# Fill and emptying of a three-stage pipeline over groups: vectors loaded as rows, two groups side by side at the start, the last-but-one product in pieces at the end

## The chip, the cores and the metric

One core of a Trainium2 chip. The metric is the device time of one execution in microseconds (us), median of several executions. Batches of kernels ran on one chip beside fresh runs of the kernel before, whose median was 3388.9 to 3390.4 us each time. Ratios are the mean time of one kernel's runs over the mean of the other's runs of the same rounds, so they are not quite the ratio of the medians quoted here. The experiments ran in three batches (e1 to e4, e5 to e8, e9 to e12), each on another chip, and the changed kernel in a batch before them; since the kernel before itself moved by 1.5 us between batches, a difference of under 2 us between kernels of two batches is not shown by their medians alone.

## The reference, cut to what matters

64 graphs with 256 nodes and 256 features go through a graph attention layer and then a relational attention layer, in float32.

```python
def _gat(h, adj, W, a, out_features):            # called twice
    Wh = jnp.matmul(h, W)
    e = Wh @ a[:F] + swapaxes(Wh @ a[F:], 1, 2)
    scores = jnp.where(adj > 0, leaky_relu(e, 0.2), NEG)
    return jnp.matmul(softmax(scores, axis=1), Wh)

# layer 0
h = _gat(_gat(x, adj, W1, a1), adj, W2, a2)
h = layernorm(x + h, g_ln1, b_ln1)
x = layernorm(h + relu(h @ w_ff1 + b_ff1) @ w_ff2 + b_ff2, g_ln2, b_ln2)
# layer 1: 8 heads, value matrix chosen by the edge's relation r
q, k = x @ Wq + bq, x @ Wk + bk
attn = softmax(q @ k.T / sqrt(32))
out  = sum over r of (attn * (adj == r)) @ (x @ Wv[r] + bv[r])
x = layernorm(x + out @ Wo + bo, g1, beta1)
return layernorm(x + gelu(x @ W1 + b1) @ W2 + b2, g2, beta2)
```

## The kernel before

Two graphs are a group; there are 32 groups. A `turn` works on three groups at once: the relational layer of group y, the feed-forward part of the graph layer of group y+1, and the first part of the graph layer of group y+2. The order on TensorE is the order in which the program is written; the other engines are ordered by the framework, and each then runs its list strictly in that order (the traces below show it: VectorE stands for 8.84 us at one instruction while later ones are ready).

Names in the traces: a name that ends in p is a result of TensorE that another engine then reads or copies. aTp and xTp are transposes of the adjacency and of x; xpp is the projection by W; `rows` spreads a column of scores over all rows for the softmax; hpp and ygp are the first and the second attention sum of the graph layer; h1T, h2T and h3T are transposes after a norm; h1p and yfp are the two products of a feed-forward part; qp, kp, vp, sp, po, zo and yop are the steps of the relational layer. "Half clock" is a granted TensorE clock of 0.50, as the profile's windows give it.

The loads of the weights, and the loop:

```python
def column(v, name):                 # a vector as a column: one element per partition
    t = const.tile([P, n], F32, name=name)
    nc.scalar.dma_start(t, v.rearrange("(c p) -> p c", p=P))
# weight() and row() also start their transfers from nc.scalar
...
nc.vector.tensor_tensor(wv[:, :, 1, :], wv[:, :, 1, :], wv[:, :, 0, :], ALU.subtract)
nc.vector.tensor_tensor(rbv[:, F:], rbv[:, F:], rbv[:, :F], ALU.subtract)
...
nc.gpsimd.tensor_add(rb1, rb1, rbf2); nc.gpsimd.tensor_add(rb2, rb2, rbo); nc.gpsimd.tensor_add(rb3, rb3, rbt2)
...
def turn(y_, x_, z):
    hT = to_features(Y["y"], f"h2T{y_}", lg2, lb2)    # transposes; VectorE copies
    second_sums(x_)                                   # ygp, then norm
    q, k_ = queries_keys(y_, hT); v = values(...)     # qp, kp, vp
    h1hT = to_features(X["y"], f"h1T{x_}", lg1, lb1)
    # scores (sp) and applied (po, zo) of y between blocks of x's hidden product (h1p)
    early(z)                                          # aTp, xTp
    out_(0); project(z); out_(1); first_scores(z)     # yop, xpp, rows
    yf = hidden_out(x_, ...)                          # yfp of the graph layer
    hT = to_features(yn, f"h3T{y_}", lg3, lb3)
    Z["hp"] = gat_first(z, ...)                       # hpp
    h1 = hidden(y_, 1, hT, ...); second_scores(z)     # h1p of the relational layer, rows
    yf = hidden_out(y_, 1, h1, w2, res)               # yfp of the relational layer
    # norm, affine, one store for all four blocks of the group

for u in range(-2, NG):
    turn(u, u + 1, u + 2)            # turns -2 and -1: fill; turns 30 and 31: emptying
```

## Time and profile before

| | us |
|---|---|
| median of 4 runs | 3389.53 |
| span of the profiled run | 3388.5 |
| 32 steady turns of 102.31 | 3273.9 |
| everything else (start, fill, emptying, tail) | 114.6 |

The steady turns have no gap on TensorE, so the table's last row is all that the change can touch. A turn's start is read from the first transpose named h2T of its group in TensorE's timeline: 224.7 us for turn 1. The prediction below shows the page, the waits and ScalarE's queue. Here is the last turn of the kernel before, from TensorE's timeline; the columns are start, duration, engine, line, operation, out<-in, shape, count, and in brackets the idle time ahead of it with what ended it.

```profile
3322.71 1.94 PE L724 MATMUL po<-e,v 128*32 128x256 f32 x16 [6.72 <-DVE oT L734]
...
3333.98 3.63 PE L617 MATMUL yop<-wo,oT 128*128 128x256 f32 x8 [2.69 <-DVE oT L734]
3341.24 2.21 PE L540 MATMUL h3T31p<-ident,yo 128*128 128x128 f32 x8 [3.63 <-DVE yo L637]
3343.50 16.01 PE L655 MATMUL h1p<-h3T,w 128*128 128x512 f32 x32
```

Three waits for VectorE, and after them matmuls that run wholly or partly at half clock (0.50 in the windows from 3322 to 3326 and from 3342 to 3346 us): yop takes 3.63 us where it otherwise takes 1.89, and h1p 16.01 where it otherwise takes 13.90.

### The profile page before, as it was taken

The numbers are of one execution on the slowest core, as the hardware profiler recorded it, in microseconds if no ns is written. First come the engines' busy times: TensorE is split into PE (matmuls) and PEld (weight loads), VectorE is DVE, ScalarE is ACT, GpSimd is POOL, SyncE is SP. The second block draws the span as 40 slices with busy tenths as digits, with TensorE's granted clock in tenths as the row PEclk, the third lists the DMA queues.
The fourth block names the chain that finished last, engine by engine and source line by source line (L and its number), as shares of the span: only waits on it lengthen the run. The fifth ranks groups of instructions, "written<-read, shape, count | busy, mean of one in ns | idle before, by whom it ended". The sixth has DMA issues, their size and how long they took to land.

```text
span 3388.5 us, 43264 instructions
## 1 busy us (share of the span) xinstructions
PE 3304.7 (98%) x17946; PEld 2164.6 (64%) x17946; DVE 1820.3 (54%) x3607; ACT 1083.8 (32%) x1920; POOL 986.0 (29%) x844
## 2 busy tenths in 40 slices
PE   5899999999999999999999999999999999999996
PEld 3566666666666666666666666666666666666654
DVE  2545565545565555565455565455665455655444
ACT  1323333323323323323323333323333233333221
POOL 1233232332232332322332322332322332323321
PEclk7999999999999999999999999999999999999998
DMA  4000000000000000000000000000000000000000
GB/s 123 13 20 13 13 19 19 13 19 7 19 20 20 13 19 7 19 20 19 13 19 7 20 19 20 13 19 7 20 19 14 19 17 9 19 19 7 7 7 8
DMA packets 62458, 60.92 MB, mean 18 GB/s; under 512 B 7216, under 2 KB 61616, under 8 KB 62256
## 3 DMA queue, kind: packets, MB, share of 16 engines
q1 hardware_dynamic: 33792, 33.56, 3.1%
q0 software_dynamic: 16896, 16.78, 2.2%
q10 hardware_dynamic: 11568, 7.76, 0.9%
q8 instruction: 143, 2.34, 0.3%
q14 instruction: 59, 0.48, 0.0%
HBM read 41.31 MB, written 16.78 MB: 17 GB/s over the span
## 4 chain that ended last, share of the span: by engine, by line
PE 96%; DVE 1%; ACTq 1%; DMA 0%; issue 0%; POOL 0%; ACT 0%; POOLq 0%; DVEq 0%
PE h1p L655 27%; PE yfp L617 26%; PE po L724 7%; PE vp L687 6%; PE sp L703 4%; PE yop L617 3%; PE hpp L606 3%; PE kp L674 3%; PE ygp L617 3%; PE qp L674 3%; PE xpp L568 3%; PE zo L727 2%; PE rows L578 1%; PE aTp L555 1%; ACTq L462 1%
## 5 line engine op out<-in xcount | busy, mean ns | idle before, releaser
L655 PE MATMUL h1p<-h1T,wf 128*128 128x512 f32 x1024 | 474.6, 607 | 0.1
L655 PE MATMUL h1p<-h3T,w 128*128 128x512 f32 x1024 | 447.2, 595 | 1.0 <-DVE h3T L544 0.9
L617 PE MATMUL yfp<-wf,h 128*128 128x256 f32 x2048 | 447.3, 379 | 0.0
L617 PE MATMUL yfp<-w,h 128*128 128x256 f32 x2048 | 447.3, 379 | 0.0
L711 DVE TENSOR_TENSOR ea<-e,aT 128x1024 f32<-128x1024 f32 x256 | 320.2, 1291 | 195.2 <-ACT e L709 195.2
L617 PEld LDWEIGHTS yfp<-w,h 128*128 128x128 f32 x2048 | 386.8, 190 | 52.2 <-issue 1.0
L617 PEld LDWEIGHTS yfp<-wf,h 128*128 128x128 f32 x2048 | 386.7, 190 | 51.3
L709 ACT ACTIVATE e<-sp 128x512 f32<-128x512 f32 x512 | 264.3, 603 | 298.6 <-PE sp L703 298.6
L655 PEld LDWEIGHTS h1p<-h3T,w 128*128 128x128 f32 x1024 | 195.1, 191 | 234.4 <-issue 229.8
L733 POOL TENSOR_TENSOR low<-low,rz 128x512 f32<-128x512 f32 x64 | 82.2, 1284 | 880.3 <-DVE rz L732 880.3
L655 PEld LDWEIGHTS h1p<-h1T,wf 128*128 128x128 f32 x1024 | 184.9, 190 | 232.8 <-issue 190.9
L587 DVE SCALAR_TENSOR_TENSOR s<-s 128x512 f32<-128x512 f32 x128 | 90.2, 706 | 442.5 <-ACT s L584 441.3
L620 DVE TENSOR_TENSOR yf<-yfp,res 128x512 f32<-128x512 f32 x128 | 88.5, 692 | 424.9 <-PE yfp L617 423.8
L645 POOL TENSOR_TENSOR res<-res,rb 128x1024 f32<-128x1024 f32 x128 | 301.4, 2354 | 10.0
L657 ACT ACTIVATE h<-h1p,bf 128x512 f32<-128x512 f32 x256 | 177.3, 693 | 282.9 <-PE h1p L655 282.9
L657 ACT ACTIVATE h<-h1p,b 128x512 f32<-128x512 f32 x256 | 175.8, 687 | 258.7 <-PE h1p L655 257.5
L633 POOL TENSOR_TENSOR rs<-ve,mhalf 128x4 f32<-128x4 f32 x128 | 130.8, 1022 | 408.2 <-DVE ve L632 408.2
L732 DVE RECIPROCAL rz<-zo 128x512 f32<-128x512 f32 x64 | 214.6, 3354 | 63.8 <-PE zo L727 63.8
L687 PE MATMUL vp<-wv,h2T 128*128 128x512 f32 x512 | 230.1, 592 | 0.0
L676 ACT ACTIVATE q<-qp,bq 128x512 f32<-128x512 f32 x64 | 44.0, 688 | 530.8 <-PE qp L674 530.8
L608 ACT COPY hp<-hpp 128x258 f32<-128x258 f32 x128 | 48.0, 375 | 441.7 <-PE hpp L606 441.7
L644 POOL TENSOR_TENSOR res<-yf,rg 128x1024 f32<-128x1024 f32 x64 | 150.8, 2356 | 95.8 <-DVE yf L637 94.3
(486 smaller groups left out, 4393.1 us busy)
## 6 DMA issues: line engine op xcount, KB each, us to landing
xs<-in_x_dram SPq DMA_DIRECT2D x32, 512.0 KB, 3.9
af<-in_adj_dram POOLq DMA_DIRECT2D x32, 512.0 KB, 4.4
out_dram<-res SPq DMA_DIRECT2D x32, 512.0 KB, 2.9
wf<-in_L_gnn_w_ff_dram ACTq DMA_DIRECT2D x2, 1024.0 KB, 10.6
w<-in_L_gnn_W_dram ACTq DMA_DIRECT2D x2, 1024.0 KB, 9.6
wv<-in_L_gnn_Wv_dram ACTq DMA_DIRECT2D x2, 256.0 KB, 4.6
gw<-in_L_gnn_W_dram ACTq DMA_DIRECT2D x1, 256.0 KB, 4.5
gw2e<-in_L_gnn_W_dram ACTq DMA_DIRECT2D x1, 256.0 KB, 6.8
```

The costliest lines, as they stand in the source:

```text
L617: nc.tensor.matmul(ps[:, i * F:(i + 1) * F], lhs(t, k), rhs(b, k), start=(k == 0), stop=(k == n - 1))
L644: nc.gpsimd.tensor_mul(r, xn, g[:, None, :].to_broadcast([P, T, F]))
L645: nc.gpsimd.tensor_add(r, r, b[:, None, :].to_broadcast([P, T, F]))
L655: nc.tensor.matmul(ps, wi[:, k, f * P:(f + 1) * P], hT[:, k, :], start=(k == 0), stop=(k == KB - 1))
L657: nc.scalar.activation(h1[:, f, :], ps, func, bias=bi[:, f:f + 1])
L674: nc.tensor.matmul(ps, w[:, k, m * P:(m + 1) * P], hT[:, k, :], start=(k == 0), stop=(k == KB - 1))
L687: nc.tensor.matmul(ps, hT[:, k, t * P:(t + 1) * P], wvf[:, k, :], start=(k == 0), stop=(k == KB - 1))
L703: nc.tensor.matmul(ps[a][:, j * N:(j + 1) * N], k_[hp, m, j0:j0 + P], q[hp, m, b * N:(b + 1) * N], start=True, stop=True)
L709: nc.scalar.activation(e[:, a, :], ps[a], AF.Exp, scale=isd)
L711: nc.vector.tensor_tensor(ea[:, a:a + 2, :], e[:, a:a + 2, :], ab[:, None, :].to_broadcast([P, 2, NB * N]), ALU.mult)
L724: nc.tensor.matmul(po[hp, m * N:(m + 1) * N], vs[:, hp], w[:, a, j * N:(j + 1) * N], start=(n == 0), stop=(n == len(terms) - 1))
L732: nc.vector.reciprocal(rz, zo)
```

## The change

Its intent: take away what the two ends of the pipeline lose.

1. Loads. Vectors that were loaded as columns come as contiguous rows, twelve of them, and two small TensorE transposes turn them. Weights and bias rows are issued by SyncE instead of ScalarE. Group 1's data are loaded at once.
2. Fill. Groups 0 and 1 go through the first part of the graph layer side by side, so that the softmax of one can lie beside the matmuls of the other.
3. Emptying. Turn 30 does not do its last product; turn 31 does it in four pieces, at places where it used to wait.
4. Tail. The last group's sum, norm, affine and store are done for each half.

```diff
-        nc.scalar.dma_start(t, w.rearrange("(c p) f -> p c f", p=P))
+        nc.sync.dma_start(t, w.rearrange("(c p) f -> p c f", p=P))
...
-    def column(v, name):
-        nc.scalar.dma_start(t, v.rearrange("(c p) -> p c", p=P))
+    def columns(vs, name, queue):
+        for v, n in zip(vs, ns):
+            queue.dma_start(rows[at:at + n, :], v.rearrange("(c p) -> c p", p=P))
+        nc.tensor.transpose(ps[:, :at], rows[:at, :], ident[:at, :at])
+        nc.vector.tensor_copy(t, ps[:, :at])
...
+    def out_pieces(u, h1, res):          # a generator: one block of yfp per call,
+        ...                              # after two blocks: add, norm, affine, store
...
+                yield piece, None        # in turn(): ahead of apply 0 and of apply 2 ...
+            piece()                      # ... ahead of yop(1) and of h3T
...
+        if y_ == NG - 2:
+            left.append(out_pieces(y_, h1, res))
+        elif y_ == NG - 1:
+            for _ in out_pieces(y_, h1, res):
+                pass
...
-        for u in range(-2, NG):
+        for stage in (early, project, first_scores):
+            stage(0)
+        for stage in (early, project, first_scores):
+            stage(1)
+        for stage in (first_sums, second_scores):
+            stage(0)
+        for stage in (first_sums, second_scores):
+            stage(1)
+        second_sums(0)
+        hT = to_features(g[0]["y"], "h1T0", lg1, lb1)
+        h1 = hidden(0, 0, hT, wf1, bf1, AF.Relu, range(FB))
+        yf = hidden_out(0, 0, h1, wf2, g[0]["res"])
+        ...
+        second_sums(1)
+        for u in range(NG):
             turn(u, u + 1, u + 2)
```

More of the change, by code (lines that the diff above doesn't have):

```diff
@@ L429, in load @@
         nc.sync.dma_start(xs, x[G * u:G * (u + 1)].rearrange("b (c p) f -> p (b c) f", p=P))
-        af = io.tile([P, T, N], F32, tag="af", name=f"af{u}", bufs=1)
+        if u == 1:
+            af = work.tile([P, FB, TN], F32, tag="h1", name=f"af{u}", bufs=1)
+            af = af[:, 0:2, :].rearrange("p c (t n) -> p (c t) n", t=2)
+        else:
+            af = io.tile([P, T, N], F32, tag="af", name=f"af{u}", bufs=1)
         nc.gpsimd.dma_start(af, adj[G * u:G * (u + 1)].rearrange("b (c p) f -> p (b c) f", p=P))
         return xs, af
-    loaded = {0: load(0)}
     ident = const.tile([P, P], F32, name="ident")
@@ L455, in weight @@
         t = const.tile([P, w.shape[0] // P, w.shape[1]], F32, name=name)
-        nc.scalar.dma_start(t, w.rearrange("(c p) f -> p c f", p=P))
+        nc.sync.dma_start(t, w.rearrange("(c p) f -> p c f", p=P))
         return t
-    def column(v, name):
-        n = v.shape[0] // P
-        t = const.tile([P, n], F32, name=name)
-        nc.scalar.dma_start(t, v.rearrange("(c p) -> p c", p=P))
-        return t
+    def columns(vs, name, queue):
+        ns = [v.shape[0] // P for v in vs]
+        rows = work.tile([P, KB * N], F32, tag="rz", name=f"{name}r")[:, 0:P]
+        t = const.tile([P, sum(ns)], F32, name=name)
+        at, views = 0, []
+        for v, n in zip(vs, ns):
+            queue.dma_start(rows[at:at + n, :], v.rearrange("(c p) -> c p", p=P))
+            views.append(t[:, at:at + n])
+            at += n
+        ps = bank(f"{name}p")
+        nc.tensor.transpose(ps[:, :at], rows[:at, :], ident[:at, :at])
+        nc.vector.tensor_copy(t, ps[:, :at])
+        return views
     def row(v, name):
@@ L467, in row @@
         t = const.tile([P, n], F32, name=name)
-        nc.scalar.dma_start(t, bass.AP(tensor=v.tensor, offset=v.offset, ap=[[0, P], [1, n]]))
+        nc.sync.dma_start(t, bass.AP(tensor=v.tensor, offset=v.offset, ap=[[0, P], [1, n]]))
         return t
@@ L475, in gat_weights @@
         w2e = work.tile([P, KB, WX], F32, tag="wh", name="gw2e")
-        nc.scalar.dma_start(w2e[:, :, :F], g_W2.rearrange("(c p) f -> p c f", p=P))
-        a1 = column(g_a1.rearrange("f o -> (f o)"), "ga1")
-        a2 = column(g_a2.rearrange("f o -> (f o)"), "ga2")
+        nc.sync.dma_start(w2e[:, :, :F], g_W2.rearrange("(c p) f -> p c f", p=P))
+        a1, a2 = columns([v.rearrange("f o -> (f o)") for v in (g_a1, g_a2)], "ga", nc.scalar)
         def transposed(w, name):
@@ L506, in narrow_path @@
     gwe = gat_weights()
+    g = {u: {} for u in range(NG)}
+    for u in range(2):
+        g[u]["xs"], g[u]["af"] = load(u)
     wf1, wf2 = weight(g_wf1, "wf1"), weight(g_wf2, "wf2")
-    bf1 = column(g_bf1, "bf1")
-    lg1, lb1 = column(g_g1, "lg1"), column(g_b1, "lb1")
-    lg2, lb2 = column(g_g2, "lg2"), column(g_b2, "lb2")
+    lg1, lb1, bf1, lg2, lb2, bq, bk, lg3, lb3, b1 = columns(
+        (g_g1, g_b1, g_bf1, g_g2, g_b2, t_bq, t_bk, t_g1, t_be1, t_b1), "cols", nc.scalar)
     rg1, rb1, rg2, rb2 = row(g_g1, "rg1"), row(g_b1, "rb1"), row(g_g2, "rg2"), row(g_b2, "rb2")
@@ L514, in narrow_path @@
     wq, wk, wo = weight(t_Wq, "wq"), weight(t_Wk, "wk"), weight(t_Wo, "wo")
-    bq, bk = column(t_bq, "bq"), column(t_bk, "bk")
     wv = const.tile([P, KB, 2, F], F32, name="wv")
     for r in range(2):
-        nc.scalar.dma_start(wv[:, :, r, :], t_Wv[r].rearrange("(c p) f -> p c f", p=P))
+        nc.sync.dma_start(wv[:, :, r, :], t_Wv[r].rearrange("(c p) f -> p c f", p=P))
     rbv = row(t_bv[0:2].rearrange("r f -> (r f)"), "rbv")
@@ L523, in narrow_path @@
     w1, w2 = weight(t_W1, "w1"), weight(t_W2, "w2")
-    b1 = column(t_b1, "b1")
-    lg3, lb3 = column(t_g1, "lg3"), column(t_be1, "lb3")
     rg3, rb3, rg4, rb4 = row(t_g1, "rg3"), row(t_be1, "rb3"), row(t_g2, "rg4"), row(t_be2, "rb4")
@@ L621, in add_blocks, with normed @@
                                 res[:, bt, :].rearrange("p t f -> p (t f)"), ALU.add)
-    def normed(u, l, y):
-        st = work.tile([P, T, 6], F32, tag="st", name=f"st{u}_{l}")
-        mv = work.tile([P, T, 2], F32, tag="mv", name=f"mv{u}_{l}")
-        ve = work.tile([P, T], F32, tag="ve", name=f"ve{u}_{l}")
-        rs = work.tile([P, T], F32, tag="rs", name=f"rs{u}_{l}")
-        for t in range(T):
+    def normed(u, l, y, blocks=range(T)):
+        n, t0 = f"{u}_{l}_{blocks[0]}", blocks[0]
+        bt = slice(t0, t0 + len(blocks))
+        st = work.tile([P, T, 6], F32, tag="st", name=f"st{n}")
+        mv = work.tile([P, T, 2], F32, tag="mv", name=f"mv{n}")
+        ve = work.tile([P, T], F32, tag="ve", name=f"ve{n}")
+        rs = work.tile([P, T], F32, tag="rs", name=f"rs{n}")
+        for t in blocks:
             nc.vector.bn_stats(st[:, t, :], y[:, t, :])
             nc.vector.bn_aggr(mv[:, t, :], st[:, t, :])
-        nc.vector.tensor_scalar(ve, mv[:, :, 1], EPS, None, op0=ALU.add)
-        nc.gpsimd.tensor_tensor(rs, ve, mhalf, ALU.pow)
+        nc.vector.tensor_scalar(ve[:, bt], mv[:, bt, 1], EPS, None, op0=ALU.add)
+        nc.gpsimd.tensor_tensor(rs[:, bt], ve[:, bt], mhalf[:, bt], ALU.pow)
         if l == 3:
-            nc.gpsimd.tensor_add(high, high, mv[:, :, 0])
-        for t in range(T):
+            nc.gpsimd.tensor_add(high[:, bt], high[:, bt], mv[:, bt, 0])
+        for t in blocks:
             nc.vector.tensor_scalar(y[:, t, :], y[:, t, :], mv[:, t, 0:1], rs[:, t:t + 1],
@@ L639, in normed, with affine @@
         return y
-    def affine(u, l, xn, g, b):
-        r = work.tile([P, T, F], F32, tag="res", name=f"res{u}_{l}", bufs=3)
-        nc.gpsimd.tensor_mul(r, xn, g[:, None, :].to_broadcast([P, T, F]))
-        nc.gpsimd.tensor_add(r, r, b[:, None, :].to_broadcast([P, T, F]))
+    def affine(u, l, xn, g, b, r=None):
+        if r is None:
+            r = work.tile([P, T, F], F32, tag="res", name=f"res{u}_{l}", bufs=3)
+        nc.gpsimd.tensor_mul(r, xn, g[:, None, :].to_broadcast(list(r.shape)))
+        nc.gpsimd.tensor_add(r, r, b[:, None, :].to_broadcast(list(r.shape)))
         return r
@@ L736, in divided @@
                                 rz.rearrange("p (m n) -> p m n", m=KB), ALU.mult)
-    g = {u: {} for u in range(NG)}
     def early(z):
@@ L770, in second_sums, with piece @@
         d["res"] = affine(x_, 0, d["y"], rg1, rb1)
+    left = []
+    def out_pieces(u, h1, res):
+        y = work.tile([P, T, F], F32, tag="y", name=f"yf{u}_1")
+        r = work.tile([P, T, F], F32, tag="res", name=f"res{u}_3", bufs=3)
+        for b in range(G):
+            ps = bank(f"yfp1_{u}_{b}")
+            for i in range(NB):
+                t = b * NB + i
+                for k in range(FB):
+                    nc.tensor.matmul(ps[:, i * F:(i + 1) * F], h1[:, k, t * P:(t + 1) * P], w2[:, k, :],
+                                     start=(k == 0), stop=(k == FB - 1))
+                if i == NB - 1:
+                    bt = slice(b * NB, (b + 1) * NB)
+                    nc.vector.tensor_tensor(y[:, bt, :].rearrange("p t f -> p (t f)"), ps,
+                                            res[:, bt, :].rearrange("p t f -> p (t f)"), ALU.add)
+                    normed(u, 3, y, range(b * NB, (b + 1) * NB))
+                    affine(u, 3, y[:, bt, :], rg4, rb4, r[:, bt, :])
+                    nc.sync.dma_start(out[G * u + b].rearrange("(c p) f -> p c f", p=P), r[:, bt, :])
+                yield
+    def piece(_=None):
+        if left:
+            next(left[0], None)
     def turn(y_, x_, z):
@@ L774, in have @@
             return 0 <= u < NG
+        if y_ == 0:
+            g[z]["xs"], g[z]["af"] = load(z)
         if z + 1 < NG:
@@ L780, in turn @@
             hT = to_features(Y["y"], f"h2T{y_}", lg2, lb2)
-        if have(x_):
+        if have(x_) and y_ > 0:
             second_sums(x_)
@@ L822, in steps @@
                 yield scores, 3
+                yield piece, None
             yield hid, range(6, 8)
@@ L852, in turn @@
             res = affine(y_, 2, yn, rg3, rb3)
+            piece()
         if have(x_):
@@ L864, in turn @@
             second_scores(z)
-        if have(y_):
+        if y_ == NG - 2:
[3 more added lines that the diff above has]
+                pass
+        else:
             yf = hidden_out(y_, 1, h1, w2, res)
@@ L869, in turn, with first_sums @@
             nc.sync.dma_start(out[G * y_:G * (y_ + 1)].rearrange("b (c p) f -> p (b c) f", p=P), res)
-    g[0]["xs"], g[0]["af"] = loaded.pop(0)
+    def first_sums(z):
+        g[z]["hp"] = gat_first(z, g[z]["s"], g[z]["xp"])
     with tc.manual_schedule(engines={mybir.EngineType.PE}):
-        for u in range(-2, NG):
+        for stage in (early, project, first_scores):
[10 more added lines that the diff above has]
+        yf = hidden_out(0, 0, h1, wf2, g[0]["res"])
+        g[0]["y"] = normed(0, 1, yf)
+        g[0]["res"] = affine(0, 1, g[0]["y"], rg2, rb2)
+        second_sums(1)
+        for u in range(NG):
             turn(u, u + 1, u + 2)
```

## The prediction

> **What bounds the kernel now.** I read the page first, then TensorE's waits, its timeline at both ends, the ScalarE queue beside it, and the clock by window.
>
> ```profile
> span 3388.5 us, 43264 instructions
> PE 3304.7 (98%) x17946; PEld 2164.6 (64%) x17946; DVE 1820.3 (54%) x3607; ACT 1083.8 (32%) x1920; POOL 986.0 (29%) x844
> PE   5899999999999999999999999999999999999996
> ...
> PEclk7999999999999999999999999999999999999998
> ...
> PE 96%; DVE 1%; ACTq 1%; DMA 0%; issue 0%; POOL 0%; ACT 0%; POOLq 0%; DVEq 0%
> ```
>
> TensorE is the bound: 98% busy, 96% of the chain that ended last. Only the first two or three slices and the last one are not full. In the middle the same group step recurs: h2T1p starts at 224.70 us and h2T30p at 3191.66, so 29 turns take 2966.96, or 102.31 us each, with TensorE busy in every microsecond of the windows from 200 to 3200 and a clock of 1.00. The change leaves these matmuls as they are, so all it can win is outside 32 x 102.31 = 3273.9 us: 3388.5 - 3273.9 = 114.6 us. I split that:
>
> - before the first matmul of a group (aTp at 16.37): **16.4**
> - fill: turn 1 starts at 224.70. Before it lie one full turn (102.3) and the parts of earlier turns: twice the first part of a group (aTp 0.87, xTp 0.97, xpp 3.50, rows 0.44, hpp 3.49, rows 0.44 = 9.7) and once the middle part (ygp 3.45, h1T 0.88, first hidden 14.4, yfp 13.8 = 32.6): 154.3 at full rate. 224.7 - 16.4 - 154.3 = **54.0** lost
> - emptying: turns 30 and 31 run from 3191.6 to 3373.3, 181.7 us, for 92.6 + 60.0 = 152.6 of work: **29.1** lost, 24.4 of it in turn 31
> - tail, last matmul to end: **15.2**
>
> ```profile
> PE rows L578 <- ACT xp L570: 17.8, 1, 17.8
> PE ygp L617 <- POOL hp L596: 12.9, 2, 8.0
> PE goodp L887 <- DVE good L885: 6.9, 1, 6.9
> PE po L724 <- DVE oT L734: 6.7, 1, 6.7
> PE yop L617 <- DVE oT L734: 5.5, 2, 2.8
> PE gw1tp L485 <- DMA gw<-in_L_gnn_W_dram: 5.5, 1, 5.5
> PE hpp L606 <- POOL xp L596: 4.9, 1, 4.9
> PE h3T31p L540 <- DVE yo L637: 3.6, 1, 3.6
> PE h1T0p L540 <- DVE yg L637: 3.6, 1, 3.6
> ```
>
> These waits (total, times, longest) are nearly all of TensorE's idle time, and all fall in the fill or the emptying. The longest waits for ScalarE, which was issuing transfers until 38.3 us:
>
> ```profile
> 5.34 3.85 ACTq L462 DMA_DIRECT2D bf<-in_L_gnn_b_ff_dram  x1
> 9.22 3.53 ACTq L462 DMA_DIRECT2D lg<-in_L_gnn_g_ln_dram  x1
> ...
> 29.35 5.33 ACTq L462 DMA_DIRECT2D lg<-in_L_gnn_g_dram  x1
> ...
> 38.32 1.28 ACT L557 ACT_TABLE_LOAD   x1 [38.32 <-DMA rg<-in_L_gnn_g_dram]
> ```
>
> **What the Trainium skill says.** "DMA: Bandwidth & Descriptors", Rules for kernel authors: a non-contiguous last dimension becomes one descriptor per element. The trace agrees: issuing a 1 KB column held ScalarE for 0.6 to 5.33 us, a contiguous 128 KB row 0.44. The same page, Issuing engines are not separate DMA queues: another issuer saves issue time only, the 16 engines are shared. So moving the weights to SyncE frees ScalarE but does not bring them sooner. "TensorE: Matmul & The Clock Gate", Part 1: an idle window of about 3.4 us halves the clock. Here the window 30 to 35 us shows 0.50, and after the 6.7 us wait of po its 16 matmuls take 1.94 us where they otherwise take 1.07. "SBUF — State Buffer", Who interferes with whom: a VectorE instruction with two SBUF inputs and a GpSimd one that reads SBUF block each other for a whole instruction. Here a 128x1 product (good) took 2.15 us beside GpSimd's res, where other 128x1 instructions took 0.15.
>
> **The change, part by part.**
>
> *Loading.* The column issues on ScalarE add up to 22 us; they become twelve contiguous ones, about 0.5 us each, beside gw1. ScalarE should be free near 8 us instead of 38.3. Two small transposes and copies per kernel are added, under 1 us. VectorE stood until 9.94 for the ga column, which held gwap to 11.22; with ga and gw2e sooner, aTp of group 0 starts near 14.5: saves **1.9**.
>
> *Fill.* The work before turn 1 stays 154.3. Groups 0 and 1 interleaved, by my walk through the new order:
> - xT copies before each projection: 2 x 1.1 (the row xpp <- xT)
> - hp takes the buffer of xp (two buffers, both groups alive), so its four copies (0.38 each) begin only after the last product of the group: about 1.8 twice = 3.6, where the kernel before copied during the products
> - softmax: rows end to first hpp took 4.9; beside it there are now the other group's 9.7 or 3.9 us of matmuls, so about 1.5 remains once
> - norm and transposes between ygp(0) and the first hidden product: ends at 64.70, starts at 70.62, 5.9 with about 1.3 of work: 4.6, not covered
> - start of turn 0 (norm of yf, h2T copies), partly under ygp(1): 1.4
> - half clock after the gaps: before some 12 of the 54 (hpp 5.25 for 3.64, ygp 6.57 and 5.86 for 3.5, h1T 2.3 for 0.9, and so on); now 4
> - late weights: GpSimd's three row sums and VectorE's wv difference sit in these engines' queues and wait for transfers. By 16 us before had moved 4.2 MB; about 10 MB with group 1's 1 MB in front, at the 120 to 360 GB/s of the windows, put wv and rbv near 29 us and the last rows near 38. The products hpp could begin at about 29. If the wv difference stands ahead of group 0's softmax, they start 3 to 5 later; if the last row sum does, 10. I can't see these engines' order, so I take 5.
>
> Sum 22.3. Turn 1 then starts at 14.5 + 154.3 + 22.3 = 191.1 instead of 224.7: **33.6 saved**, the 1.9 included.
>
> *Emptying.* Turn 30's last product, 64 matmuls of 13.8 us, is cut into four pieces of 3.45 inside turn 31. I count gaps and cold clock in turn 31: 24.4 (po 6.7, yop 2.7, h3T31p 3.6, small waits 1.4, and 10 of slow matmuls such as h1p 16.0 for 13.7). A piece stands before apply 2 (it covers about half of the 6.7, because VectorE's chain of ea, es and the 3.35 us reciprocal gets 2.6 of add and norm for group 30 too), one before yop(1) (2.7 covered) and one before h3T (3.45 of 3.6). So some 4 of waits, 2 of VectorE delay and 4 of clock remain, about 10: **14.4 saved**. Turn 30 keeps its 4.7.
>
> *Tail.* From 3373.35: add 0.69, statistics and variance 1.0, power and high 1.2, four scalings 1.38, multiply 2.35, add 2.34, issue and landing about 3, and about 3 of ending. For half of the rows the scalings save 0.7, multiply and add 1.15 each, the landing some 0.2: **3.2 saved**.
>
> Total 33.6 + 14.4 + 3.2 = 51.2. **3390.2 - 51.2 = 3339.**
>
> **The rivals.**
>
> *A. Weights take ScalarE's place as the wait.* For it: before, VectorE waited 9.5 us for wv and GpSimd 14.9 for rb, in order, with no harm only because ScalarE was later still. If both engines block, first products start near 40 and the gaps cool the clock: fill saves 25 only, the time is about 3348. If neither blocks and the idles are small, the fill saves 41: 3331.
>
> *B. The pieces displace rather than fill.* In turn 31 VectorE runs without a gap from 3310.7 to 3322.6. If the scheduler puts group 30's adds and norms ahead of ea and es, or GpSimd's affine blocks ea at the shared port, TensorE waits after the pieces as long as before: emptying saves 8 instead of 14.4, 3346.
>
> *C. All works, nearly no gap left.* The gain is bounded: with 5 of loss in turn 31, a fill loss of 12 and a tail of 12, 3327. Even then 2% (66.5 us) is missed. For 2%, more than half of the whole 114.6 would have to go, and the 14 us at the start and 12 at the end can't.
>
> *D. The middle changes.* The list of matmuls is the same and TensorE had no gaps in it; 0.1 us per turn would be 3 us. The new order in the norm's names shouldn't do that.
>
> **Range and chances.** A and B together give about 3355, C 3327. I take 3328 to 3353 for 8 in 10. Faster by over 2%: 0.04, for an error in my split of the ends. Slower by over 2% needs the steady turns to break: 0.01. Within 2%: 0.95.
>
> **What would show each step.** ScalarE's table load near 8 us instead of 38.3. The wait rows <- ACT xp (17.8) gone. The second start of h2T (group 1) near 191, read from the timeline. VectorE's wait for wv or GpSimd's for rb ending before the first hpp would show rival A to be small; hpp starting after 38 would show it whole. Copies of hp that all follow the last hpp matmul of their group. 102.3 us between further starts of h2T. Then pieces of yfp between sp and po in turn 31, h1p of the last group at 13.7 to 14.5 instead of 16.0, and some 12 us from the last yfp matmul to the end. Wrong would be: turns of another length, a first hpp before 27 or after 42, or a wait in turn 31 that is longer than 6.7.

## The result, and the profile after

3345.38 us median (3344.66 to 3346.05, 4 runs) against 3389.53 (3387.83 to 3391.59, 4 runs); ratio 0.9869, 95% interval 0.9852 to 0.9887. That is 44 us shorter, within 2%, inside the predicted range and 6.4 us above the predicted 3339.

The page:

```profile
span 3342.7 us, 43294 instructions
PE 3298.2 (99%) x17948; PEld 2160.2 (65%) x17948; DVE 1818.6 (54%) x3611; ACT 1083.8 (32%) x1920; POOL 987.4 (30%) x852
PE   7999999999999999999999999999999999999998
```

TensorE's slices at both ends are fuller than before. Its busy time fell by only 6.5 us (less half clock), its idle time by 39. The waits of TensorE, the fill first:

```profile
PE xpp L578 <- DVE xT L552: 8.7, 2, 7.7
PE h1T0p L550 <- DVE yg L649: 5.2, 1, 5.2
PE yop L627 <- DVE oT L747: 2.8, 1, 2.8
PE po L737 <- DVE oT L747: 2.7, 1, 2.7
PE qp L687 <- DVE h2T L554: 2.6, 2, 2.1
```

The wait of 17.8 for ScalarE is gone. The longest of the fill is now one that was 1.1 before: xpp of group 1 waits 7.65 us for VectorE. Its timeline says why:

```profile
32.22 5.82 PE L578 MATMUL xpp<-gwe,xT 128*128 128x260 f32 x16 [7.65 <-DVE xT L552]
...
97.08 5.40 PE L687 MATMUL qp<-h2T,wq 128*128 128x512 f32 x8 [2.05 <-DVE h2T L554]
...
196.86 1.04 PE L550 MATMUL h2T1p<-ident,yf 128*128 128x128 f32 x8
```

and VectorE's, at the same time:

```profile
27.48 0.69 DVE L533 TENSOR_TENSOR wv<-wv 128x512 f32<-128x512 f32 x1 [8.84 <-DMA wv<-in_L_gnn_Wv_dram]
```

VectorE stood for 8.84 us at the difference of the two value matrices, whose transfer had not landed, with group 0's softmax and xT of group 1 behind it in its list. xpp then ran mostly at half clock (0.50 from 32 to 36 us; 5.82 us, 3.67 at full clock). Turn 1 starts at 196.86.

The last turn after, in the same lines as above:

```profile
3282.93 1.94 PE L737 MATMUL po<-e,v 128*32 128x256 f32 x16 [2.75 <-DVE oT L747]
...
3290.64 3.62 PE L794 MATMUL yfp<-w,h 128*128 128x256 f32 x16
3294.09 1.89 PE L627 MATMUL yop<-wo,oT 128*128 128x256 f32 x8
3295.82 3.62 PE L794 MATMUL yfp<-w,h 128*128 128x256 f32 x16
3299.62 1.64 PE L550 MATMUL h3T31p<-ident,yo 128*128 128x128 f32 x8 [0.18 <-DVE yo L649]
```

po's wait fell from 6.72 to 2.75, h3T's from 3.63 to 0.18, and yop starts with no wait: one piece of yfp lies ahead of it, and one ahead of h3T. h1p afterwards takes 14.3 in two parts instead of 16.0.

The losses outside the steady turns, split as the prediction does (turn starts from TensorE's timeline; work of 154.3 in the fill and 152.6 in turns 30 and 31, as there):

| | before | predicted | after |
|---|---|---|---|
| start, to the first matmul of a group | 16.4 | 14.5 | 14.3 |
| fill | 54.0 | 22.3 | 28.2 |
| emptying, turns 30 and 31 | 29.1 | 14.7 | 13.8 |
| tail | 15.2 | 12.0 | 12.5 |
| sum | 114.6 | 63.4 | 68.8 |

Start, emptying, tail and the length of a turn (102.31 still) came out within a microsecond. The miss is the fill, 5.9 us too long. (Parts are rounded, so a column may differ from its sum by 0.1.)

### The profile page after: what moved, and what is told of

The parts are those of the page before. It is cut to its first block, busy times and chain, and to the rows that moved or that the text cites. A ratio compares the mean times of both kernels' runs of the same rounds, so it can differ in the third digit from the quotient of the medians.

```text
span 3342.7 us, 43294 instructions
## 1 busy us (share of the span) xinstructions
PE 3298.2 (99%) x17948; PEld 2160.2 (65%) x17948; DVE 1818.6 (54%) x3611; ACT 1083.8 (32%) x1920; POOL 987.4 (30%) x852
## 2 busy tenths in 40 slices
DMA packets 57258, 60.92 MB, mean 18 GB/s; under 512 B 1976, under 2 KB 56416, under 8 KB 57056
## 4 chain that ended last, share of the span: by engine, by line
PE 97%; DVE 1%; issue 1%; DMA 1%; POOL 0%; SPq 0%; ACT 0%; ACTq 0%; POOLq 0%; DVEq 0%
PE h1p L668 27%; PE yfp L627 25%; PE po L737 7%; PE vp L700 7%; PE sp L716 4%; PE yop L627 3%; PE qp L687 3%; PE hpp L616 3%; PE xpp L578 3%; PE kp L687 3%; PE ygp L627 3%; PE zo L740 2%; PE rows L588 1%; PE aTp L565 1%; PE yfp L794 1%
## 5 line engine op out<-in xcount | busy, mean ns | idle before, releaser
L670 ACT ACTIVATE h<-h1p,cols 128x512 f32<-128x512 f32 x512 | 353.2, 690 | 531.7 <-PE h1p L668 530.5
L627 PE MATMUL yfp<-w,h 128*128 128x256 f32 x1920 | 419.4, 379 | 0.0
L627 PEld LDWEIGHTS yfp<-w,h 128*128 128x128 f32 x1920 | 362.5, 190 | 48.1
L658 POOL TENSOR_TENSOR res<-res,rb 128x1024 f32<-128x1024 f32 (+1 forms) x130 | 301.3, 2317 | 10.2
L645 POOL TENSOR_TENSOR rs<-ve,mhalf 128x4 f32<-128x4 f32 (+1 forms) x130 | 131.6, 1012 | 411.9 <-DVE ve L644 411.8
L689 ACT ACTIVATE q<-qp,cols 128x512 f32<-128x512 f32 x64 | 44.0, 687 | 530.4 <-PE qp L687 530.4
L657 POOL TENSOR_TENSOR res<-yf,rg 128x1024 f32<-128x1024 f32 (+1 forms) x66 | 151.2, 2291 | 96.2 <-DVE yf L649 95.4
L700 PEld LDWEIGHTS vp<-wv,h2T 128*128 128x128 f32 x512 | 94.9, 190 | 107.6 <-issue 107.6
```

What stands on the lines that cost most here:

```text
L627: nc.tensor.matmul(ps[:, i * F:(i + 1) * F], lhs(t, k), rhs(b, k), start=(k == 0), stop=(k == n - 1))
L657: nc.gpsimd.tensor_mul(r, xn, g[:, None, :].to_broadcast(list(r.shape)))
L658: nc.gpsimd.tensor_add(r, r, b[:, None, :].to_broadcast(list(r.shape)))
L670: nc.scalar.activation(h1[:, f, :], ps, func, bias=bi[:, f:f + 1])
L700: nc.tensor.matmul(ps, hT[:, k, t * P:(t + 1) * P], wvf[:, k, :], start=(k == 0), stop=(k == KB - 1))
```

## The experiments

The theory: the fill's extra loss is VectorE's place in line behind wv, and other in-order effects of putting two groups side by side. Rivals: GpSimd's row sums, which also wait for transfers; or the fill's gain has nothing to do with the interleave. All kernels were correct. "T1" is the start of turn 1 in the profile.

| run | median us | range | ratio to before | T1 |
|---|---|---|---|---|
| changed kernel | 3345.38 | 3344.66–3346.05 | 0.9869 | 196.9 |
| e1_wv_late | 3340.68 | 3337.70–3342.32 | 0.9858 | 190.7 |
| e2_both_late | 3340.36 | 3340.03–3341.14 | 0.9855 | 191.5 |
| e3_old_columns | 3348.90 | 3347.69–3350.31 | 0.9882 | 200.5 |
| e4_weights_act | 3358.07 | 3356.74–3358.86 | 0.9908 | 210.2 |
| e5_old_fill | 3355.63 | 3354.09–3356.33 | 0.9898 | 208.0 |
| e6_no_pieces | 3361.17 | 3360.66–3362.39 | 0.9915 | 197.7 |
| e7_whole_tail | 3347.47 | 3346.71–3347.94 | 0.9874 | 197.8 |
| e8_norm_order | 3340.54 | 3339.30–3341.42 | 0.9855 | 192.3 |
| e9_softmax_after | 3337.79 | 3336.51–3338.10 | 0.9847 | 188.4 |
| e10_fill_order | 3335.83 | 3333.45–3336.15 | 0.9840 | 186.4 |
| e11_own_buffers | 3335.70 | 3334.32–3336.05 | 0.9841 | 186.3 |
| e12_all_sums_late | 3328.90 | 3327.79–3330.11 | 0.9822 | 181.4 |

### What do the late weights cost?

**e1_wv_late**: the two differences are queued behind the last softmax of the fill.

```diff
-    nc.vector.tensor_tensor(wv[:, :, 1, :], wv[:, :, 1, :], wv[:, :, 0, :], ALU.subtract)
-    nc.vector.tensor_tensor(rbv[:, F:], rbv[:, F:], rbv[:, :F], ALU.subtract)
...
+        with tc.issue_after(last[1, 1, 'z']):    # reciprocal of group 1's second softmax
+            (the same two lines)
```

> The changed kernel with one thing moved: VectorE's differences of wv and rbv are queued behind the softmax of both groups instead of ahead of it. Theory (VectorE stands in order before late weights): the 7.7 us wait of xpp for xT of group 1 and the half clock after it (2.1 us) go, xpp of group 1 starts near 25.5 us instead of 32.2, turn 1 starts near 190 instead of 196.9, the time is about 7 us shorter (3338.5). Rival (the wait only passes to GpSimd's last row sum, which stands between the scalings of xp of groups 0 and 1 until the last row lands near 35): less than 3 us gained, hpp of group 1 still after 41. Second rival (group 1's x or adj lands late): xpp still starts near 32.

Measured: 4.7 us shorter by the medians, and turn 1 6.2 us earlier. The profiled run was the fastest of four that spread over 4.6 us, so the trace shows more than the median. Both lie above the rival's bound of 3. TensorE's timeline:

```profile
27.56 3.93 PE L576 MATMUL xpp<-gwe,xT 128*128 128x260 f32 x16 [2.95 <-DVE xT L550]
```

The wait fell from 7.65 to 2.95 and xpp runs at nearly full clock: 4.7 + 1.9 = 6.6 us. The other 2.95 is not wv's: xT1's copies stand in VectorE's list behind the softmax of group 0. The move has a price of its own: VectorE now does the two differences inside group 0's norm (at 49.20 and 50.03 us), and h1T waits 6.09 us where it waited 5.23.

**e2_both_late**: GpSimd's three row sums are queued late as well.

```diff
-    nc.gpsimd.tensor_add(rb1, rb1, rbf2)    # and rb2, rb3
+        with tc.issue_after(last[0, 1, 'wh']):   # group 0's second scaling; rb3: group 1's
+            nc.gpsimd.tensor_add(rb1, rb1, rbf2)
```

> As e1_wv_late, and GpSimd's three row sums are queued behind the scalings too. Theory: with e1 most is gained, here another 1 to 3 us (hpp of group 1 near 35), time about 3337. Rival (GpSimd's row sum takes over the whole wait): e1 gains nearly nothing and this one gains 6 or more beyond it.

Measured: no further gain (0.3 us, T1 0.8 later); the expected 1 to 3 us did not come. In e1 hpp of group 1 already starts right behind `rows`, so GpSimd's sums held nothing on TensorE; queued late, they stand in group 0's norm (h1T waits 7.02 instead of 6.09). In this order of the fill the sums' early place costs nothing. That holds for this order only: see e12.

### What was the new loading worth, and which half of it?

**e3_old_columns**: vectors element by element as before, still on ScalarE; weights on SyncE.

```diff
-            queue.dma_start(rows[at:at + n, :], v.rearrange("(c p) -> c p", p=P))
+            queue.dma_start(t, v.rearrange("(c p) -> p c", p=P))
```

> The changed kernel with the vectors loaded as columns again, element by element, from ScalarE; weights stay on SyncE. Theory (issue of element-wise columns holds ScalarE): ScalarE's table load is at 20 to 26 us instead of 10.0, gwap waits for ga until 10 or later, but a part is hidden because VectorE stands until 28.4 anyway: 3 to 6 us longer than the changed kernel, near 3350. Rival (what held ScalarE was the weights' queue, columns are cheap without them): table load before 14 us and less than 1 us longer.

**e4_weights_act**: vectors as rows, but weights and bias rows issued by ScalarE as before.

```diff
-        nc.sync.dma_start(t, w.rearrange("(c p) f -> p c f", p=P))
+        nc.scalar.dma_start(t, w.rearrange("(c p) f -> p c f", p=P))
```

> The changed kernel with the weights and broadcast rows issued from ScalarE again; vectors stay rows with transposes. Theory (ScalarE is also held by the back-pressure of the big loads: SyncE's issues ended at 29.6 us): table load near 30 us instead of 10.0, turn 1 near 205 instead of 196.9, about 8 us longer, 3353. Rival (only columns mattered): table load before 16 and less than 2 us longer.

Measured: the columns alone cost 3.5 us, the queue alone 12.7, more than expected. ScalarE's first own work, the load of its function table, is the mark for when its issuing is over: 38.32 us before, 10.02 after. In e3 and in e4:

```profile
15.86 1.28 ACT L561 ACT_TABLE_LOAD   x1 [15.86 <-DMA cols<-in_L_gnn_g_dram]
```

```profile
29.78 4.11 ACTq L480 DMA_DIRECT2D rg<-in_L_gnn_g_dram  x1
...
35.77 1.28 ACT L567 ACT_TABLE_LOAD   x1 [35.77 <-DMA w<-in_L_gnn_W_dram]
```

With the vectors as rows and the weights still on ScalarE, it is free only 2.5 us sooner than in the kernel before. The issue times in ScalarE's timelines say more. The columns' add up to 21.8 us in the kernel before, to 11.7 in e3, where the weights go through SyncE, and as rows to 3.6 in the changed kernel. So about half of what the columns seemed to cost came with the weights in the same queue, and most of ScalarE's 38 us was not the columns' own. In e4 all issues together take 25.2 us, and another 9.7 pass between issues, for a reason that no view names. The contiguous row rg, whose issue takes 0.44 us at other times, held ScalarE for 4.11 while the core's transfers moved 368 GB/s, just behind the issues of two weights of 1 MB. The runs show the hold, not the mechanism behind it.

e3 shows the other half of the columns' cost. They slow other issuers as well: SyncE's two issues of wf took 9.40 us there,

```profile
6.61 9.40 SPq L459 DMA_DIRECT2D wf<-in_L_gnn_w_ff_dram  x2
```

against 3.84 in the changed kernel, and the stretch from 12 to 16 us moved 173 GB/s instead of 356. VectorE therefore got wv at 31.64 instead of 27.48 us, and xpp of group 1 waited 11.63. A smaller part came at the start, where gwap waited for ga and the first aTp came at 15.44 instead of 14.33. The expectation for e3 had the table load at 20 to 26; it was 15.86, so the expected cost came by another path, through the weights.

### What was the interleave worth?

**e5_old_fill**: loads, pieces and split tail stay; the fill goes back to turns −2 and −1.

```diff
-        (the fifteen lines that take groups 0 and 1 side by side)
-        for u in range(NG):
+        for u in range(-2, NG):
             turn(u, u + 1, u + 2)
```

> The changed kernel with the order of the fill of the kernel before (group 0 through its graph layer alone, group 1's first part within group 0's hidden product); loads, pieces and split ending stay. In the kernel before, 183.7 us passed from the first rows (41.0) to turn 1 (224.7). Here rows is at about 22 and VectorE's wait for wv (to 28.4) delays the softmax by some 5. Theory (side by side covers softmax waits of one group with the other's matmuls): turn 1 near 211 instead of 196.9, 14 us longer than the changed kernel, 3359. Rival (the loads alone gave the fill's gain, the interleave nothing): turn 1 before 200 and less than 3 us longer.

Measured: 10.3 us longer, T1 11.1 later. The rival, that the loads alone did it, is out. The theory is right in kind; its 14 was too much. The waits that the interleave covers are back, and with them the half clock (hpp otherwise takes 3.66):

```profile
30.78 6.69 PE L611 MATMUL hpp<-xp,s 128*128 128x258 f32 x16 [7.79 <-POOL xp L601]
...
104.51 5.65 PE L622 MATMUL ygp<-hp,s 128*128 128x256 f32 x16 [8.00 <-POOL hp L601]
```

So of the 27.8 us by which turn 1 came forward, 16.7 (224.7 − 208.0) are there with the loads alone and 11.1 came with the interleave.

### What were the pieces and the split tail worth?

**e6_no_pieces**:

```diff
-        if y_ == NG - 2:
-            left.append(out_pieces(y_, h1, res))
-        elif y_ == NG - 1:
+        if y_ == NG - 1:
```

> The changed kernel, but turn 30 does its last product itself, as the kernel before did; the last group keeps its split ending. Theory (the pieces fill real gaps of turn 31, whose loss was 24.4 us before and 9.2 after): 14 to 15 us longer, near 3360, with po's wait of 6.7 and h3T31p's of 3.6 back. Rival (pieces mostly displace, VectorE's chain ends when it ends): less than 8 us longer.

Measured: 15.8 us longer; po's wait is 6.72 again and h3T's 3.63, to the hundredth the values of the kernel before. Turns 30 and 31 together took 182.1 us against 166.4, and turn 31 alone 84.9 without the pieces and 83.0 with them. So the pieces filled gaps: turn 31 did not grow by any of their 13.8 us.

**e7_whole_tail**:

```diff
-        elif y_ == NG - 1:
-            for _ in out_pieces(y_, h1, res):
-                pass
```

> The changed kernel with the last group's sum, norm, affine and store for all four blocks at once, as before. Theory: last yfp matmul to the end 15.2 us instead of 12.5, so 2.7 to 3 us longer, 3348.3. Rival (the end is set by the check of the flags and the branch, not by the stores): under 1 us.

Measured: 2.1 us longer; 14.5 us from the end of yfp to the end of the span, instead of 12.5. So the rival is out, and the last group's chain of sum, norm, affine and store sets the end; which of the four, this run does not separate.

### Can the rest of the fill's loss be had?

**e8_norm_order**: e1, with group 0's sums and norm written ahead of group 1's second softmax, and group 1's sums left in their banks until h2T of group 0 is copied.

```diff
+        first_sums(1)
         second_sums(0)
+        second_scores(1)
...
-        second_sums(1)
+        sums_products(1)         # matmuls only; added in turn 0 behind h2T's copies
```

> e1_wv_late with two more reorderings of the fill: group 0's second sums and norm come before group 1's second softmax on VectorE and GpSimd; and group 1's sums stay in their banks until VectorE has copied h2T of group 0. Theory (interleaving costs in the in-order engines: h1T waits 6.1 us in e1 where the kernel before waited 3.6, and h2T's copies stand 2.1 us behind group 1's sums, with half clock after): h1T waits about 3.6, the wait of qp for h2T falls under 0.7 and qp takes 3.6 instead of 5.4: turn 1 near 185 instead of 190.7, about 5.5 us shorter than e1, near 3335. Rival (TensorE then waits elsewhere, for group 1's softmax or its own banks): less than 2 us.

Measured: 0.1 us shorter than e1, and the two ran in different batches, so no difference; T1 1.6 later. The expectation failed and the rival held. The second part worked: qp waits 0.55 instead of 2.06 and takes 3.70 instead of 5.40. The first part made a new wait, of 4.70 us ahead of h1p. VectorE and GpSimd in e8:

```profile
53.25 2.56 DVE L600 SCALAR_TENSOR_TENSOR s<-s,aT 128x256 f32<-128x256 f32 x1
...
55.74 2.55 DVE L600 SCALAR_TENSOR_TENSOR s<-s,aT 128x256 f32<-128x256 f32 x1
...
58.22 0.80 DVE L552 TENSOR_SCALAR h1T<-h1T0p,cols 128x512 f32<-128x512 f32 x1
```

```profile
53.08 2.46 POOL L657 TENSOR_TENSOR res<-yg,rg 128x1024 f32<-128x1024 f32 x1 [1.50 <-DVE yg L649]
55.61 2.40 POOL L658 TENSOR_TENSOR res<-res,rb 128x1024 f32<-128x1024 f32 x1
```

Writing the softmax later put it into the middle of group 0's norm rather than behind it. Two of its mask multiplies, 0.42 us elsewhere, lasted as long as GpSimd's two passes beside them, and h1T's copies stood behind. The 1.6 us of T1 should not be read as a loss by the edit: xpp of group 1 took 5.62 us here and 3.93 in e1, after nearly the same wait (3.09 and 2.95).

**e9_softmax_after**: e1, with group 1's second softmax queued behind h1T's copies.

```diff
         hT = to_features(g[0]["y"], "h1T0", lg1, lb1)
+        with tc.issue_after(last["h1T0"]):
+            second_scores(1)
```

> e1_wv_late with one reordering: group 1's second softmax comes behind VectorE's two copies of h1T of group 0, so that it runs beside group 0's hidden product instead of ahead of it or (e8) between its norm and its copies. In e1 8.4 us pass from the end of group 0's ygp (46.3) to the first h1p (54.7), in e8 8.2 with the first h1p waiting 4.7 for h1T behind mask multiplies that took 2.55 us instead of 0.42. Theory (e8 failed because the softmax was moved only from before the norm to the middle of it): with nothing of group 1 in between, ygp's end to h1p takes 5.5 to 6 as in the kernel before, no wait of h1p for h1T over 1 us, turn 1 near 187.7, 3 us shorter than e1, 3337.5. Rival (GpSimd's own hp scaling and affine set it, not VectorE's order): less than 1 us.

Measured: 3337.79, 2.9 us shorter than e1, T1 2.3 earlier; h1T's wait is 3.66 instead of 6.09. That is the expected result. One run of e1 lies within e9's range, so the trace carries it:

```profile
50.42 2.21 PE L550 MATMUL h1T0p<-ident,yg 128*128 128x128 f32 x8 [3.66 <-DVE yg L649]
```

The norm's excess came from VectorE's order; 0.9 us of it were e1's own, since e9 also takes the two differences out of the norm. T1 understates the gain: xpp of group 1 took 5.62 us at half clock (0.50 from 28 to 30 us) behind a wait of 2.99, and 3.93 in e1 behind one of 2.95.

**e10_fill_order**: e9, both groups' transposes ahead of the first projection, and sums in banks as in e8.

```diff
+        early(0)
+        early(1)
-        for stage in (early, project, first_scores):
+        for stage in (project, first_scores):
             stage(0)
```

> e9_softmax_after plus two more: both groups' transposes come before the first projection (so xT1's copies stand ahead of group 0's softmax on VectorE; in e1 xpp of group 1 waits 2.95 for them, xpp of group 0 1.06), and group 1's sums stay in their banks until h2T of group 0 is copied (e8: wait of qp 0.55 instead of 2.06 and qp at 3.70 instead of 5.40). Theory: hpp of group 0 starts near 28.8 instead of 32.1 (3.3 us), qp saves 3.3, turn 1 near 181, 6.5 us shorter than e9, near 3331. Rival (the waits only move on to the next in-order engine, as in e8): less than 3 us shorter than e9.

Measured: 2.0 us shorter than e9, so by its own bound the rival held. xpp no longer waits at all and hpp of group 0 starts at 27.69, 4.95 us sooner than in e9 (32.64; 1.95 of it because xpp is at full clock again), but all of that is lost again at group 1's hpp: ygp starts at 43.92, in e9 at 43.02. What stays is the 3.0 us of qp (wait 0.55 instead of 2.05, then 3.70 instead of 5.19), less this 0.9. TensorE:

```profile
38.68 5.40 PE L616 MATMUL hpp<-xp,s 128*128 128x258 f32 x16 [4.96 <-POOL xp L606]
```

and GpSimd:

```profile
37.10 0.72 POOL L539 TENSOR_TENSOR rb<-rb,rbt 128x256 f32<-128x256 f32 x1 [6.69 <-DMA rb<-in_L_gnn_beta_dram]
```

This is the row sum that e2 had found harmless. Now that VectorE is no longer late, GpSimd's stand in line shows.

**e11_own_buffers**: e10, with hp of groups 0 and 1 in two buffers that are idle in the fill, to test the prediction's term for hp's buffer.

```diff
+        if u < 2:
+            hp = work.tile([P, T, 2 * F], F32, tag=("v", "ea")[u], name=f"hp{u}", bufs=1 + u)[:, :, :WX]
```

> e10_fill_order, and groups 0 and 1 put hp into two buffers that are idle in the fill (those of v and ea), so hp's copies need not wait for a slot of the ring that xp and hp share. Theory of the prediction (its term of 3.6 us for hp's buffer): in e1 rows waits 0.52 twice on ScalarE's hp copies, which follow hpp directly anyway, so the buffer costs little: under 1 us. Rival (the ring holds hp until xp's readers are done, and the prediction's 3.6 us are there): 2 us or more shorter than e10.

Measured: 0.1 us shorter. rows no longer waits 0.53 for hp's copies, but hpp of group 1 then waits 6.07 for GpSimd instead of 4.96. So here the buffer is worth nothing; what it would be worth without GpSimd's wait is open.

**e12_all_sums_late**: e10 with GpSimd's row sums queued late, as in e2.

> e10_fill_order plus GpSimd's three row sums queued behind its scalings (as in e2). In e10 group 1's row sums were ready at 31.3 but GpSimd stood 6.69 us in order (30.4 to 37.1) for the load behind the third row sum, so xp of group 1 was scaled only from 38.1 and hpp of group 1 waited 4.96; that is where the expected 6.5 us of e10 went, of which 2 were seen. In e2 the same sums did not matter, because VectorE's own wait ended later. Theory: hpp of group 1 follows group 0's rows at once near 33.7 at full clock (3.67 instead of 5.40); then group 0's second softmax sets the start of ygp, near 40.3 instead of 43.9: turn 1 near 182.8, 3.6 us shorter than e10, near 3332. Rival (group 0's softmax and scaling set ygp's start anyway): less than 1 us.

Measured: 3328.90, 6.9 us shorter than e10; T1 5.0 earlier. hpp of group 1 follows rows at once and ygp starts at 38.14:

```profile
33.07 3.66 PE L613 MATMUL hpp<-xp,s 128*128 128x258 f32 x16
38.14 3.74 PE L624 MATMUL ygp<-hp,s 128*128 128x256 f32 x16 [1.41 <-POOL hp L603]
```

That is more than the expected 3.6. ygp's start came 5.8 us forward (43.92 to 38.14) instead of 3.6: the expectation put it behind all four of group 0's scalings, but GpSimd began these at 37.61 and ygp started 0.5 us later, before they were done. A further 1.7 us of the profiled difference cannot be put down to the edit, which touches only the fill: turn 30 took 85.1 us in the profile of e10 and 83.4 in that of e12. (Turn 31 differs by another 0.8, also in matmuls after a wait: 83.2 and 82.4.) In e10:

```profile
3205.07 2.64 PE L627 MATMUL yop<-wo,oT 128*128 128x256 f32 x8 [2.79 <-DVE oT L747]
3207.50 15.04 PE L627 MATMUL yfp<-wf,h 128*128 128x256 f32 x64
```

and in e12:

```profile
3200.09 1.96 PE L624 MATMUL yop<-wo,oT 128*128 128x256 f32 x8 [2.79 <-DVE oT L744]
3201.89 13.98 PE L624 MATMUL yfp<-wf,h 128*128 128x256 f32 x64
```

The wait is the same 2.79 us, and once half clock follows it (0.50 from 3207 to 3208 us) and once it does not (1.00 throughout). Twelve profiles have this wait in turn 30 (e6's has a longer turn): the turn took 83.4 in those of the changed kernel, e1, e3, e4, e5, e7, e8 and e12, and 85.1 in those of e2, e9, e10 and e11. Differences of under 2 us between single profiles should be read with that in mind.

e12 is the version that beats both: 60.7 us below the kernel before, ratio 0.9822 (0.9806 to 0.9839), still within 2%. Its losses are 14.1 at the start, 13.0 in the fill, 13.2 in the emptying and 12.3 in the tail, 52.6 in all.

## Why the prediction was right or wrong

**Right: the bound.** TensorE is the bound, the middle stays at 102.31 per turn, and only 114.6 us could be touched. Rival D (the middle changes) is refuted by the turns' length.

**Right: the emptying.** 14.4 predicted from gaps that the pieces can lie in; e6 shows 15.8, the traces 15.3 (29.1 to 13.8). Rival B (the pieces displace) is refuted by e6. Turn 31 loses 9.2, not the 10 that were left to it; no run says which of the three parts of that 10 was too large.

**Right, slightly over: the tail.** 3.2 predicted; 2.7 in the traces, 2.1 in e7.

**Wrong in its reason: why ScalarE was late.** The prediction put 22 of ScalarE's 38.3 us down to the columns ("The column issues on ScalarE add up to 22 us") and counted on rows to free it. It read issue times of 0.6 to 5.33 us as a sign of transfers element by element. Such transfers are there (packets under 512 B: 7216 before, 7249 in e3, 1976 after; the twelve vectors have 5120 elements), but with the weights on SyncE the columns' issues take 11.7 us, and a contiguous row can take 4.11 (e4). The table load near 8 came out at 10.02, but e4 shows that rows on the same queue would have left it at 35.77. Moving the weights off ScalarE was the larger part: 12.7 us against 3.5 for the columns. That the forecast did not suffer is luck: the change does both.

**Wrong in size: the fill's sum, 22.3 predicted, 28.2 measured.** Term by term, from the timelines and the runs:

| term | predicted | measured |
|---|---|---|
| late weights (wv on VectorE) | 5 | 6.9: 4.7 of wait, 2.2 of half clock; 6.2 by e1 |
| xT copies before the projections | 2.2 | 4.0: 1.06 for group 0, 2.95 for group 1 behind group 0's softmax |
| hp's buffer | 3.6 | 2.5 at this place (two waits of 0.52, slow `rows`); that it is the buffer is not shown (e11) |
| softmax, uncovered rest | 1.5 | 0 |
| norm and transposes ahead of the hidden product | 4.6 | 6.9 |
| start of turn 0 | 1.4 | 2.9 |
| half clock elsewhere | 4 | 3.7 |
| not assigned (small slow matmuls) | – | 1.3 |

The mechanism of rival A was there, for VectorE: 4.7 us by the medians, 6.2 by T1, against the 3 to 5 that the prediction gave for this case. GpSimd's sum, feared at 10, cost nothing in this order (e2 against e1). By the prediction's own sign ("hpp starting after 38 would show it whole") rival A was there whole, since the first hpp started at 38.66; the fill's gain of 27.8 lies between rival A's 25 and the 33.6. But the sign does not single out the late weights: in e1, without VectorE's wait for them, hpp still starts at 32.12 and not at the 29 that the prediction took. Two terms that the prediction counted only as a single group's were larger for the same reason: xT1's copies stood behind group 0's softmax, and group 0's norm stood behind group 1's softmax and scalings. The prediction counted what the interleave covers on TensorE and left out what it puts in line on VectorE and GpSimd. e9 took back 2.3 us of T1 for the norm (e1 had added 0.9 us to the norm's wait), e10 the waits of xpp, and e8 and e10 those of turn 0.

**The fill's gain, split.** The predicted 33.6 for start and fill together came out at 27.8. By e5 the interleave gave 11.1 of it, the loads 16.7. The prediction had not split this.

**Still open.** Why an issue is held while large transfers are under way; what fills the time between ScalarE's issues in e4; what decides whether some 2.8 to 3 us of idle time brings half clock; and what hp's own buffer would be worth in e12's order.

## What to carry to other kernels

When two groups are put side by side, count the order on each in-order engine and not only the cover on the bound one: an operation that waits for a transfer belongs behind everything that doesn't need it, on every engine, but not inside the next chain that TensorE waits for (e1's two differences landed in group 0's norm), and the second such wait only shows when the first is gone (e2 against e12). Issue large loads from an engine with no work of its own; rows instead of columns help, but here the queue was worth more than three times as much (12.7 against 3.5 us). At the end of a pipeline, keep back a product that is ready and lay it in pieces where the last group waits; that worked here to within 1.4 us of an estimate made from the gaps alone.

## What the Trainium skill lacked or had wrong

- "DMA: Bandwidth & Descriptors", Issuing engines are not separate DMA queues: it says that issuing from another engine only saves the sequencer's time, "usually small relative to the DMA itself". Here another issuer was worth 12.7 us (e4): the sequencer's time was not small, since an issuer can be held while big transfers are under way (a contiguous row took 4.11 us to issue instead of 0.44). The section also doesn't say that element-wise transfers lengthen the issues of another engine: wf's issue on SyncE took 9.40 us beside them and 3.84 without (e3).
- "TensorE: Matmul & The Clock Gate", Part 1: it gives an idle window of about 3.4 us as what halves the clock. Here a wait of 2.79 us was followed by half clock in four of the twelve profiles that have it (turn 30 of 85.1 instead of 83.4 us), and one of 2.99 in e9's fill, so staying under 3.4 us is not enough to keep the clock.
